# The zeroing of layer 1's expert slots, spread over more of the kernel

## The chip, the cores and the metric

One core of a Trainium2 chip runs the whole program: TensorE (PE; its weight loads are shown apart as PEld), VectorE (DVE), ScalarE (ACT), GpSimd (POOL), SyncE (SP), and 16 DMA engines that all of them feed. The metric is the time of one execution in device microseconds, here the median of several. An engine carries out its own instructions in order and waits by semaphore for what another one makes. A DMA is issued by SP, ACT or POOL and runs beside; whoever needs its data waits for its landing.

## The reference, cut to what matters

Two layers over `x` of 4 batches of 1024 tokens with 256 features, all in float32. Each layer norms its input, computes a sequence part `s` and a routed mixture of experts `g`, and adds `s * silu(g)`:

```python
xn = _layernorm(x)
s = _L0_attn_ref(xn, ...)             # a minimal GRU, a scan along the sequence
g = _silu(_L0_ffn_ref(xn, ...))       # 16 experts, hidden 128, 4 per token
x = x + s * g
xn = _layernorm(x)
s = _L1_attn_ref(xn, ...)             # attention over cos(theta) * cos(xn)
g = _silu(_L1_ffn_ref(xn, ...))       # 16 experts, hidden 64, 4 per token, plus a shared expert
x = x + s * g
```

The router takes, for each token, the two best of four groups of experts and then the four best experts in these; their scores, divided by their sum, weigh the four results.

## The kernel before

**Slots.** The tokens of an expert are brought together in DRAM. A group of tokens has an array `rows_in` with one row for each slot; an expert's tokens take whole tiles of 128 slots, so the number of slots is fixed and some stay empty. POOL scatters each token's row into its four slots with indirect DMAs (`scattered`, L577: 128 rows in one DMA). The expert loop then loads four tiles at a time (a quad), multiplies, and puts the results back. Layer 0 has two such groups of tokens (`HALVES`, 64 and 96 tiles), layer 1 has two as well (`GROUPS`, batches 0 and 1, then 2 and 3; 80 tiles each). The code numbers them 0, 1 and `G1` = 2, 3.

**Zeros.** Slots that no token takes must hold harmless rows, so each `rows_in` is filled before anything is scattered into it. `cleared(g, part, parts)` (L833) writes one part of a group's array from a tile of zeros, as one DMA on SP. Layer 0's two arrays are written whole, at the start. For layer 1 a row has 261 numbers (256 features, the marks of the token's four slots, and a result row; for an empty slot the last is a huge number), and an array is 10.7 MB; it is written in ten parts of 1044 KB each. `clears(10)` (L1325) yields the twenty parts one by one.

**Order of the work.** The order in which instructions stand on each engine is written by a planner in the code. A main loop (`run`, L887) advances a planning clock by a fixed amount for each of its steps (`PAIR` 0.81 for layer 0's experts, `ATTEND` 1.4, `SHARE` 2.6, `ROUTED` 0.64), and a few products of side work add their length to it (`spent`). After each step it lets side tasks go on (`Beside.advance`, L873), each of which is due again after the pause that it yields, times its pace. The clock decides the order only; nothing waits for it on the chip. The stages, with the planning clock worked out from these constants:

| stage | steps | planning clock |
|---|---|---|
| layer 0's routing, scatters, GRU | | 0 to 56.1 |
| layer 0's experts (`experts0`), 80 pairs of tiles | 333 x 0.81, and 24.3 of `spent` | 56.1 to 350.1 |
| attention and shared expert of batch 0 | 34 x 1.4 and 18 x 2.6, and 13.9 of `spent` | 350.1 to 458.4 |
| the same of batch 1 | the same, 10.3 of `spent` | 458.4 to 563.1 |
| the same of batch 2 | the same, no `spent` | 563.1 to 657.5 |
| layer 1's experts (`routed1`), 80 pairs | 0.64 a step | from 657.5 |
| shared expert and attention of batch 3 | | the end |

Beside layer 0's experts and the first three batches of attention run these tasks: `clearing` (the zeros: a part every `CLEAR` = 18.0, from 56.9 to 399.9), `combined` (it gathers layer 0's results with POOL, four indirect DMAs for 128 tokens, weighs them, L725 and L790 to L792, and writes layer 1's input), `routing` (layer 1's routing of the four batches, then `places1` of both groups, then `dispatch1(0)`, then `dispatch1(1)`), `weighing` and `preparing`.

**The scatters of layer 1.** `dispatch1(h)` first waits, in the planning clock, until all zeros have been issued (`while not clearing.done`). It then puts on POOL, for each of four pieces, a load of 512 tokens (`t_half`, L951), two small copies, and 16 scatters (L582), 20.3 planning units a piece. The last batch's routing is done at 502.3, so group `G1` is dispatched from 502.3 to 564.5 and the other group from 564.5 on. When the first is dispatched, `loads1` (L1370) puts the first three loads of layer 1's experts on SP (`xs<-rows_in`, L621), still at 564.5; these must wait until the group's scatters have landed. `weights1` (L960) follows each dispatch with 12 DVE instructions of 0.42 us for that group. Each scatter waits on the chip for every zero that was written to its own array.

**Layer 1's experts.** Each quad ends in a tile `o` of which there are three (`OB` = 3, shared by rotation). DVE writes the first half of it (L685), ACT the second (L679), and POOL stores its four tiles with four indirect DMAs (`results<-o,dest`, L1205). These stores stand behind all scatters in POOL's order. The fourth quad's first half can be written only when the first quad's stores have landed.

Of the kernel before, what the change touches and what calls it, by code (L numbers as in the profile page):

```python
# [52 lines left out]
PIECE = 1.0  # L53
# [3 lines left out]
CLEAR = 18.0  # L57
# [6 lines left out]
def two_layer_kernel(  # L64
# [33 lines left out]
    def block(dram, b, q):  # L98


        if len(dram.shape) == 4:
            return dram[b, q].rearrange("p (c d) -> p c d", c=NS)
        return dram[b].rearrange("(c p) d -> p c d", p=P)[:, q * NS : (q + 1) * NS, :]
# [383 lines left out]
    G1 = len(GROUPS)  # L487
# [89 lines left out]
    def scattered(views, tokens, row, c0):  # L577

        indirect(len(views))
        for i, view in enumerate(views):  # L580
            s, k = divmod(i, TOPK)
            nc.gpsimd.indirect_dma_start(  # L582
                out=view,
                out_offset=bass.IndirectOffsetOnAxis(ap=row[:, c0 + s, k : k + 1], axis=0),
                in_=tokens[:, s, :],
                in_offset=None,
            )
# [245 lines left out]
    def cleared(g, part, parts):  # L833


        n = NSLOT[g] // parts
        a = rows_in[g].rearrange("(p m) d -> p m d", p=P)[:, part * n : (part + 1) * n]
        source = zeros_of[g // G1].rearrange("p z d -> p (z d)")

        rows = a.rearrange("p (m z) d -> p m (z d)", z=zeros_of[g // G1].shape[1])  # L840
        nc.sync.dma_start(out=rows, in_=source.unsqueeze(1).to_broadcast(rows.shape))
# [92 lines left out]
        placed1.append((yield from places(em1[:, tiles_of(h), :], G1 + h, WE1, "tp")))  # L934

    def dispatch1(h):
        while not clearing.done:
            yield PIECE
        row, top, _ = placed1[h]
        pieces = [(b, q) for b in GROUPS[h] for q in range(NQ)]  # L940
        n = NS * TOPK
        views = dram_disjoint_views(rows_in[G1 + h], len(pieces) * n)

        tokens = {}
        for i in range(-AHEAD, len(pieces)):
            if i + AHEAD < len(pieces):
                j = i + AHEAD
                tokens[j] = t = xpool.tile([P, NS, D + INFO], F32, tag="x", name="t_half", bufs=XB)
                ts = slice(j * NS, (j + 1) * NS)
                b, q = pieces[j]  # L950
                nc.gpsimd.dma_start(out=t[:, :, 0:D], in_=block(normed, b, q))  # L951
                nc.gpsimd.tensor_copy(t[:, :, D : D + TOPK], top[:, ts, 0:TOPK])
                nc.gpsimd.tensor_copy(t[:, :, D + TOPK], result0[:, ts])
            if i >= 0:
                scattered(views[i * n : (i + 1) * n], tokens.pop(i), row, i * NS)
                while clock[0] < pool_free[0] - n * INDIRECT:
                    yield PIECE
        dispatched.add(h)
# [327 lines left out]
    stored, routed_done = set(), set()  # L1286
# [25 lines left out]
    def combine0(g):  # L1312
        while g not in stored:
            yield PIECE
        yield from gated0(g, *routed[g][0:2])
# [6 lines left out]
            yield from route1(b, tag)  # L1322
            routed_done.add(b)

    def clears(parts):  # L1325
        for g in (G1, G1 + 1):
            for i in range(parts):
                cleared(g, i, parts)
                yield CLEAR

    def then(*steps):
        for g in steps:
            yield from g

    def until(ready, *beside):

        while not ready():
# [3 lines left out]
                    other.advance(clock[0])  # L1341

    ready, turned, placed1, weights, dispatched, stored1 = {}, {}, [], [], set(), {}
    clearing = Beside(clears(10))
    combined = Beside(then(gru(xnTs[3], 3, ("side", "side"), True), *(combine0(g) for g in range(len(HALVES)))))
    routing = Beside(
        then(
            *(step for h, bs in enumerate(GROUPS) for step in (routes1(bs, "side"), places1(h))),
            *(dispatch1(h) for h in range(len(GROUPS))),
        )  # L1350
    )
# [106 lines left out]
```

## Time and profile before

| what | value |
|---|---|
| median of 3 runs | 1134.29 us (1133.79 to 1134.44) |
| the profiled execution's own time | 1132.03 us |
| its span | 1130.3 us |
| granted TensorE clock, mean | 0.957 |
| PE busy | 1029.2 us, 91% of the span |
| DVE, ACT, POOL busy | 652.7, 463.9, 564.4 us |
| zeros of layer 1 | 20 DMAs of 1044 KB, 14.5 us to landing (median) |
| gathers of layer 0's results | 128 DMAs, 6.1 us to landing (median) |
| scatters of layer 1 | 128 DMAs, 2.6 us to landing (median) |
| stores of layer 1's results | 160 DMAs, 3.3 us to landing (median) |

The profiled execution is 2.3 us below the median of the runs. A line of the timeline reads: start, length, engine, line of the kernel, operation, written tile <- read tiles, how many, and in brackets how long the engine had been idle and what ended that. `SPq` and `ACTq` are DMA issues; their length is that of the issue, not of the transfer. A line of waits reads: who waited at which line for whom: us in total, how often, the longest. Rows of the windows give the busy time (and count) of PE, PEld, DVE, ACT and POOL in a stretch, then the granted clock, the busy share of the 16 DMA engines and the GB/s moved. In the profile layer 0's experts run from about 145 to 451 us, attention and the shared expert of batches 0 to 2 from 451 to 790 us, layer 1's experts from 790 to about 1030 us.

### The profile page before, as it was taken

What the parts mean: (1) busy time and instruction counts of PE and PEld (TensorE: products, weight loads), DVE (VectorE), ACT (ScalarE), POOL (GpSimd) and SP (SyncE); (2) the same over time, 40 slices, a digit from 0 to 9 for tenths busy, and PEclk for the clock granted to TensorE, in tenths of its full rate; (3) what the DMA queues carried; (4) which work ended last, traced back from release to release, by engine and by line L of the source; (5) the groups of instructions that cost most, each with busy time, mean ns of one, the idle gap of its engine ahead of it and who ended that gap; (6) DMA issues with size and microseconds to landing.
All of it is one profiled execution on the core that took longest, in us unless ns stands there. A gap on an engine that the chain in (4) does not pass through costs nothing.

```text
span 1130.3 us, 16158 instructions
## 1 busy us (share of the span) xinstructions
PE 1029.2 (91%) x4928; PEld 765.9 (68%) x4928; DVE 652.7 (58%) x1967; ACT 463.9 (41%) x1028; POOL 564.4 (50%) x589
## 2 busy tenths in 40 slices
PE   5678699999899799979589999999999999999997
PEld 4245368888778688666357765776777777776675
DVE  4866963333688733067977884023733337776666
ACT  3345454444355444331223621221655555553132
POOL 1277377741770000377334677777756666776000
PEclk9868899999999899998699999999999999999999
DMA  8997569999999487997236553654555569994871
GB/s 338 401 410 265 172 191 324 308 310 250 313 346 263 136 215 189 342 246 196 84 119 217 181 175 130 215 196 158 179 170 186 190 215 351 359 332 145 274 242 38
DMA packets 118995, 264.82 MB, mean 234 GB/s; under 512 B 14208, under 2 KB 71680, under 8 KB 117632
## 3 DMA queue, kind: packets, MB, share of 16 engines
q1 hardware_dynamic: 78256, 138.79, 39.3%
q0 software_dynamic: 27264, 75.86, 19.9%
q10 hardware_dynamic: 13392, 49.14, 12.8%
q8 instruction: 43, 0.70, 0.3%
q14 instruction: 40, 0.33, 0.1%
HBM read 119.34 MB, written 144.39 MB: 233 GB/s over the span
## 4 chain that ended last, share of the span: by engine, by line
PE 64%; DVE 21%; DMA 7%; issue 3%; ACT 2%; POOL 2%; DVEq 0%; ACTq 0%; POOLq 0%
PE gu L642 14%; PE acc L667 10%; PE acc L1091 7%; PE tp L630 5%; PE gu L1138 4%; PE acc L1154 4%; PE mm L1138 4%; PE mm L1059 4%; DMA r<-rows_out,row 3%; PE tp L659 3%; PE acc L296 2%; DVE x_half L1243 2%; DMA rows_out<-o 2%; PE mm L514 1%; DVE stats L199 1%
## 5 line engine op out<-in xcount | busy, mean ns | idle before, releaser
L725 POOL DMA_INDIRECT r<-rows_out,row x128 | 130.6, 1021 | 237.5 <-issue 156.5
L642 PE MATMUL gu<-w_sb,xT 128*128 x1280 | 238.0, 329 | 1.5 <-ACT xT L634 0.9
L642 PEld LDWEIGHTS gu<-w_sb,xT 128*128 128x128 f32 x1280 | 193.9, 192 | 15.9 <-issue 2.2
L1205 POOL DMA_INDIRECT results<-o,dest x160 | 159.7, 998 | 76.9 <-issue 29.4
L582 POOL DMA_INDIRECT rows_in<-x_half,row x128 | 134.2, 1048 | 102.7 <-issue 52.4
L667 PE MATMUL acc<-w_sb,hT 128*128 (+1 forms) x640 | 180.1, 397 | 4.0 <-ACT hT L661 4.0
L469 DVE SCALAR_TENSOR_TENSOR h<-sg,gu 128x256 f32<-128x256 f32 (+1 forms) x160 | 56.0, 351 | 161.4 <-ACT sg L468 161.2
L582 POOL DMA_INDIRECT rows_in<-t_half,row x128 | 126.0, 985 | 40.6 <-issue 38.3
L667 PEld LDWEIGHTS acc<-w_sb,hT 128*128 128x128 f32 (+1 forms) x640 | 107.3, 189 | 31.9 <-issue 15.8
L1091 PE MATMUL acc<-val,es 128*128 128x256 f32 x512 | 127.9, 392 | 0.8 <-ACT es L1071 0.8
L634 ACT COPY xT<-tp 128x512 f32<-128x512 f32 x160 | 93.7, 586 | 73.8 <-PE tp L630 71.3
L1091 PEld LDWEIGHTS acc<-val,es 128*128 128x128 f32 x512 | 97.5, 198 | 24.3 <-issue 10.3
L630 PE MATMUL tp<-ident,xs 128*128 128x128 f32 x640 | 101.0, 281 | 0.0
L468 ACT ACTIVATE sg<-gu 128x256 f32<-128x256 f32 (+1 forms) x160 | 53.0, 331 | 113.7 <-PE gu L642 108.6
L630 PEld LDWEIGHTS tp<-ident,xs 128*128 128x128 f32 x640 | 74.4, 142 | 32.5 <-issue 18.1
L685 DVE COPY o<-acc 128x512 f32<-128x512 f32 x80 | 55.0, 688 | 61.4 <-PE acc L667 60.2
L659 PE MATMUL tp<-ident,h 128*128 128x128 f32 (+1 forms) x320 | 62.1, 276 | 10.1 <-DVE h L653 7.8
L1059 PE MATMUL mm<-projT 128*128 128x512 f32 (+3 forms) x192 | 70.0, 487 | 0.0
L661 ACT COPY hT<-tp 128x256 f32<-128x256 f32 (+1 forms) x160 | 58.5, 366 | 25.6 <-PE tp L659 23.8
L1138 PE MATMUL gu<-xnT,w_sb 128*128 128x512 f32 x128 | 61.7, 603 | 5.2 <-ACT val L1013 3.7
L1138 PE MATMUL mm<-xnT,w_sb 128*128 128x512 f32 x128 | 61.8, 608 | 0.3 <-DVE act L469 0.3
L1154 PE MATMUL acc<-w_sb,act 128*128 128x256 f32 x256 | 60.0, 380 | 1.2 <-DVE act L1148 1.2
(225 smaller groups left out, 1449.3 us busy)
## 6 DMA issues: line engine op xcount, KB each, us to landing
rows_in<-zeros SPq DMA_DIRECT2D x20, 1044.0 KB, 14.5
xs<-rows_in SPq DMA_DIRECT2D x40, 512.0 KB, 6.0
rows_out<-o ACTq DMA_DIRECT2D x40, 512.0 KB, 7.4
xs<-rows_in ACTq DMA_DIRECT2D x37, 522.0 KB, 4.0
r<-results SPq DMA_DIRECT2D x32, 512.0 KB, 5.3
rows_in<-zeros SPq DMA_DIRECT2D x1, 12288.0 KB
rows_in<-zeros SPq DMA_DIRECT2D x1, 8192.0 KB
w_sb<-in_w_dram SPq DMA_DIRECT2D x4, 1536.0 KB, 16.8
```

Source lines behind the costliest of these rows:

```text
L582: nc.gpsimd.indirect_dma_start(out=view, out_offset=bass.IndirectOffsetOnAxis(ap=row[:, c0 + s, k : k + 1], axis=0), in_=tokens[:, s, :], ...
L630: nc.tensor.transpose(tp[:, at : at + P], xs[:, j % per * 2 + i, kc * P : (kc + 1) * P], ident)
L634: nc.scalar.copy(xT.rearrange("p i k t -> p (i k t)"), tp)
L642: nc.tensor.matmul(ps[:, i * 2 * hid : (i + 1) * 2 * hid], lhsT=xT[:, i, kc, :], rhs=w_sb[:, bass.ds(off + kc * 2 * hid, 2 * hid)], start= ...
L659: nc.tensor.transpose(tp[0:hid, i * P : (i + 1) * P], h[:, i, :], ident)
L667: nc.tensor.matmul(ps[:, i * D : (i + 1) * D], lhsT=hT[0:hid, i * P : (i + 1) * P], rhs=w_sb[0:hid, bass.ds(expert(2 * j + i) + 4 * hid, D ...
L725: nc.gpsimd.indirect_dma_start(out=r[:, k, :], out_offset=None, in_=rows_out[g], in_offset=bass.IndirectOffsetOnAxis(ap=row[:, c, k : k + ...
L1059: nc.tensor.matmul(ps[:, at:TB], lhsT=projT[kc][:, t * P : (t + 1) * P], rhs=projT[kc][:, q * TB + at : (q + 1) * TB], start=(kc == 0), st ...
L1091: nc.tensor.matmul(av[s // 2][:, (s % 2) * D : (s % 2 + 1) * D], lhsT=es[:, s * P : (s + 1) * P], rhs=val[t // NS][:, t % NS, :], start=(t ...
L1138: nc.tensor.matmul(ps, lhsT=w[:, kc, j * P : (j + 1) * P], rhs=xr[:, kc, :], start=(kc == 0), stop=(kc == KC - 1),)
L1154: nc.tensor.matmul(ys[s // 2][:, (s % 2) * D : (s % 2 + 1) * D], lhsT=h[:, s * P : (s + 1) * P], rhs=ds1_sb[:, j, :], start=(j == 0 and s ...
L1205: nc.gpsimd.indirect_dma_start(out=views[g - G1][QUAD * q + i], out_offset=bass.IndirectOffsetOnAxis(ap=dest[:, i : i + 1], axis=0), in_=o ...
```

## The change

`clears` is now a task of one group. Group `G1`'s ten parts are spread at 36 planning units each; the second group's ten parts begin when layer 0's experts have been planned to their end (`1 in stored`) and the first group is through, and follow at 18 each. `dispatch1(h)` waits for the zeros of its own group (`clear_groups`) where it waited for both. The same twenty DMAs are issued, on the same queue, with the same contents.

```diff
     def dispatch1(h):
-        while not clearing.done:
+        while G1 + h not in clear_groups:
             yield PIECE
...
-    def clears(parts):
-        for g in (G1, G1 + 1):
-            for i in range(parts):
-                cleared(g, i, parts)
-                yield CLEAR
+    def clears(g, parts):
+        while g > G1 and 1 not in stored:
+            yield PIECE
+        for i in range(parts):
+            cleared(g, i, parts)
+            yield CLEAR if g > G1 else 2 * CLEAR
+        clear_groups.add(g)
...
-    clearing = Beside(clears(10))
+    clear_groups = set()
+    clearing = Beside(then(*(clears(g, 10) for g in (G1, G1 + 1))))
```

## The prediction, written before the result was known

> **What bounds the kernel now.** I read the page's slices of the span first, for where PE is not full and whether the DMA engines are full at the same time.
>
> ```profile
> PE   5678699999899799979589999999999999999997
> DMA  8997569999999487997236553654555569994871
> ```
>
> Each slice is 28.3 us. PE sets the time wherever it shows 9. In layer 0's experts (slices 5 to 15) the DMA engines are as full as PE and PE dips at slices 10 and 13; it dips again at 17, 19 and 20, where attention begins. The windows give these stretches exact edges.
>
> ```profile
> 282.00:311.00 29.00, 24.57 (x127) 20.83 (x125) 17.83 (x38) 11.39 (x27) 21.39 (x22) 0.94 1.01 308
> 370.00:396.00 26.00, 20.94 (x98) 17.53 (x97) 19.33 (x69) 11.53 (x21) 0.00 (x0) 0.87 0.54 149
> 480.00:516.00 36.00, 29.32 (x141) 24.16 (x139) 21.02 (x60) 10.04 (x30) 26.54 (x27) 0.88 0.96 254
> 535.00:571.00 36.00, 20.14 (x47) 11.47 (x45) 32.81 (x121) 10.83 (x16) 10.98 (x10) 0.76 0.24 70
> 720.00:790.00 70.00, 70.00 (x262) 47.17 (x261) 18.80 (x36) 14.98 (x40) 51.95 (x58) 1.00 0.57 200
> ```
>
> PE is idle 4.4, 5.1, 6.7 and 15.9 us in the first four rows. In the fourth DVE is full (32.8 of 36) and the DMA engines are not (0.24), so no transfer matters there. In the last PE has no gap. Next I read who waits for a transfer; first DVE's waits of 255 to 345, then those of 440 to 520.
>
> ```profile
> DVE y L792 <- DMA r<-rows_out,row: 4.1, 5, 2.3
> ```
>
> ```profile
> DVE y L792 <- DMA r<-rows_out,row: 6.8, 7, 2.8
> ```
>
> DVE waits for gathers of layer 0's results; with two short lists (0.8 at L790 there, 1.8 from 345 to 400) it is 13.5 us in all. This is what fewer zeros could shorten. Last come the queues that the change touches: SP's timeline, POOL's, and DVE's.
>
> ```profile
> 280.72 0.59 SPq L841 DMA_DIRECT2D rows_in<-zeros  x1
> ...
> 457.66 13.01 SPq L841 DMA_DIRECT2D rows_in<-zeros  x1
> ...
> 477.90 0.59 SPq L841 DMA_DIRECT2D rows_in<-zeros  x1
> ...
> 509.40 0.63 SPq L841 DMA_DIRECT2D rows_in<-zeros  x1
> ...
> 656.57 0.32 SPq L1040 DMA_DIRECT2D attended<-sv  x1
> 719.23 1.34 SPq L621 DMA_DIRECT2D xs<-rows_in  x3
> 740.87 14.30 SPq L1040 DMA_DIRECT2D attended<-sv  x2
> ```
>
> ```profile
> 716.04 0.96 POOL L582 DMA_INDIRECT rows_in<-t_half,row  x1 [0.31 <-issue]
> ...
> 722.54 1.03 POOL L582 DMA_INDIRECT rows_in<-t_half,row  x1 [2.36 <-issue]
> ...
> 804.13 0.96 POOL L582 DMA_INDIRECT rows_in<-t_half,row  x1 [0.30 <-issue]
> 805.40 0.96 POOL L1205 DMA_INDIRECT results<-o,dest  x1 [0.30 <-DVE projT L181]
> ```
>
> ```profile
> 818.07 0.69 DVE L685 COPY o<-acc 128x512 f32<-128x512 f32 x1 [1.27 <-PE acc L667]
> ...
> 831.91 0.69 DVE L685 COPY o<-acc 128x512 f32<-128x512 f32 x1 [9.55 <-PE acc L667]
> ```
>
> SP issues nothing from 657 to 719: the three tile loads of layer 1's experts wait there for the first group's last scatter (716.04). POOL is without a gap from 633 to 820: first group's scatters, the second's (722.5 to 805.1), then result stores. DVE's copy at 818.07 is the first half of the fourth quad; it needs the first quad's `o` back.
>
> **The change part by part.** The sum is made against the profiled execution, 1132.03 us, 2.3 below the median; I add the difference to the median, 1134.29.
>
> *Where the zeros come to stand.* By the planning clock the first group's ten parts start at 56.9 and follow at 36: nine stand within layer 0's experts (to 350), the tenth at 382, and the group is through at 423. They take every second place of before: 280.72 stays, 261.60 and 306.17 go; 477.90 stays, 457.66 and 509.40 go. The second group starts at 423 (just before layer 1's norm of batch 2 is stored, about 571 us) and follows at 18, with a few tenths of rounding each: part 8 at 550, part 9 at 568.7, part 10 at 586.9, through at 605. The first three tile loads are written to SP at 564.5. So two zeros come to stand behind them on SP, and the second group's scatters wait for both.
>
> *Removed from layer 0's experts and from the start of attention.* By 516 us, ten of twenty zeros are gone: 10.7 MB, at the 308 GB/s of the first window 35 us of the DMA engines. What it is worth is bounded by DVE's 13.5 us of waiting for gathers, and from below by nothing: a wait may be the gather's own latency. Of the 4.9 us before 345, nearly all falls at 294 to 301, in the wake of the zero of 280.72, which stays; of the 1.8 after 345, the zero of 343.50 goes. I take 2.0 for the two. Of the 6.8 after 440, one of the two zeros that stand there (457.66 and 477.90) goes, and SP's 13 us block at 457.66 may pass to the load behind it: half, 3.0. Sum: -5.0 us, range 0 to -13.5. The zero of 509.40 is worth nothing: DVE waits for no gather after 520.
>
> At this place a page speaks against any gain. The Trainium skill, "DMA: Bandwidth & Descriptors", section "Queues, rings and completion order", says that each DMA engine serves the queues that have work in turn, a packet at a time. By that a gather on POOL's queue would lose only a few packets to a zero on SP's, the first term would be near 0 and the sum +11.5. The chain of waits has gathers of 9.86 us (issued at 280.96) and 11.73 us (475.51) against a median of 6.1, so here more is lost, and I keep the row.
>
> *First group's own wait.* `dispatch1(0)` waits for half of the zeros now. Before, all had been issued at 509.4, and POOL's first load for it (623.51) waited 14.2 us for a DVE reader and 4.7 for a store of `normed`. Not binding: 0.
>
> *Second group's first eight zeros, beside attention.* Ten SP issues of 0.45 us move past SP's stores of `x1`, `normed` and `attended` and the reload of `xnT` (611.96). Same queue, so those land later by up to one zero, 1.07 MB or about 3.5 us. The `normed` store that POOL waits for was issued at 623.52, over 10 us after the nearest zero; `xnT` is first read at 624.61, 12.6 us after its issue. PE has no transfer on its path from 571 to 790. Cost 0; 2 us if the reload's cover is too short. Zeros 5 to 8 go out between 652 and 658, while POOL scatters; POOL's pace in the full stretch from 200 to 240 (31 in 40.2 us, 1.30 each) against 1.27 here says under 1 us.
>
> *The new wait.* Queued behind it: SP issues the three loads at 719.23, the two zeros at 720.6 and 721.0. The loads land after 8.4 us, at 728.5, sharing the engines with POOL's three loads of `normed`. The zeros follow on the same queue: 2.1 MB at 342 GB/s (the highest of the full windows, 311 to 340) is 6.2 us, so not before 734.8; with the shortest landing of that tensor, 2.4 us, 737.2. From above: the median landing of a zero, 14.5 us, on top of 728.5, 743. I take 738, near the lower end, because nothing else large moves then (DMA 0.57 in 720 to 790). The first scatter of the group moves from 722.5 to 738: 15.5 us (12.3 to 20.5). POOL's loads of `normed` stand before the waiting scatter and do not move; behind it stand 64 scatters and all 160 result stores, and all of them move by 15.5. The by-page price: "DMA: Bandwidth & Descriptors", section "Measured", gives 6.15 us for 1 MB, so two zeros end at about 741 and the sum would be about 3 us more.
>
> *Who waits for POOL.* The first quad's four stores go out from 805.40 at 1.27 each, the last at 809.2, and land 3.3 us later, 812.5. The fourth quad's copy at 818.07 has 5.6 us of margin. 15.5 - 5.6 = 9.9 us by which DVE stops, then ACT, then PE: DVE is in order, and the projections that PE's next products need (L998 at 818.95) stand behind the copy. Range 6.7 to 14.9. It is not made good: from here PE makes a quad in 5.7 us (the spacing of POOL's groups of four stores after 832) and POOL stores one in 5.07 (four times 1.27), so POOL catches up and PE, full to 1030, ends later by the stop. The second group's tile loads come only about 17 quads after 793.5, at 890, and its scatters now end at 821: 70 us of margin.
>
> *The clock after the stop.* After the gap of 4.25 us at 302.5 the next round of PE (302.54 to 307.41) took 4.87 us against 3.25 usual: +1.6. I take 1.6 here too, range 0 to 2.5. *Weights.* 12 DVE instructions of 0.42 us, 5.0 in all, move with the dispatch from batch 2's shared expert to the first quads, where DVE is busy 19.3 of 25 us (797 to 822). They lie inside the 9.9 us for which DVE would wait anyway: 0; without that wait up to 5.
>
> Sum: -5.0 + 9.9 + 1.6 = +6.5 us: 1138.5 for a profiled execution, 1140.8 for the median; I say 1140.5.
>
> **The rivals.**
>
> 1. *The stalls on gathers go whole* (faster). Place: 282 to 516 us. For it: the DMA engines show 0.95 to 1.05 there. All 13.5 us are won, and part of the granted clock of 0.94, 0.87 and 0.88, which costs 1.7, 3.4 and 4.3 us in the windows shown, say half, 4.7: -18.2 + 11.5 = -6.7, 1127.6. It decides from a gain of 11.5 us on. Against it: every second zero stays, among them those of 280.72 and 477.90.
> 2. *No new wait.* If SP took the last two zeros ahead of the tile loads, they would land before 716 and only the gain stays: 1129.3. Against it: the planning clock, 564.5 against 568.7 and 586.9, though the first margin is 4 units.
> 3. *A longer wait.* If the two zeros take the longest landing seen for one, 31.2 us from 720.6, the scatters start at 751.8, POOL is 29.3 us late and PE stops for 23.7: +20.3, 1154.6. For it: that landing occurred, with full DMA engines; against it, they are not full here.
> 4. *Gain and loss cancel.* The low end of the stop (6.7 + 1.6) and a gain of 8: 1134.6.
>
> **How the numbers follow.** About 0.2% (2.3 us) is what a measurement of this kernel can tell from no change. My forecast 0.60, with 1136.6 to 1147 as its own range (gain 8 to 2, stop 8.7 to 13); rival 1 0.10, rival 2 0.05, rival 3 0.10, rival 4 0.15. Faster 0.15, same 0.15, slower 0.70. A range from 1130 to 1150 leaves out most of rivals 1 to 3, about 0.2.
>
> **What the next profile would show.** SP: three tile loads, then two zeros at once, near 720. POOL: a gap of some 15 us between the two groups' scatters, ended by the landing of a zero; result stores from about 820. DVE: a copy at L685 that waits about 10 us for `results<-o,dest`, and PE idle as long near 820 to 830. DVE's waits for `r<-rows_out` under 13.5 us. The start of layer 1's experts a few us before 790. I am wrong if SP issues all zeros before its long wait, if the copy finds its `o` free, or if layer 0's experts end over 10 us sooner.

## The result, and the profile after

The changed kernel takes 1144.24 us (median of 4 runs, 1142.62 to 1144.91) where the kernel before takes 1134.37 beside it (1133.79 to 1135.99): a ratio of 1.0081, 95% interval 1.0058 to 1.0104. It is slower by 9.9 us; 1140.5 was predicted, with 1130 to 1150 as the range. The profiled execution took 1144.02 us (span 1142.3, granted clock 0.951), 12.0 us more than the one of before, which lies 2.3 us below its own median. The slices of the span (28.6 us each):

```profile
PE   5678699999899899987698999999699999999997
DMA  8997549988995484963477994864455668994782
```

Counted from 0, PE's dips at slices 13, 17 and 19 are a little smaller than before and the one at 10 is as it was; those at 18 and 21 are new, and so is the one at 28, in layer 1's experts. The windows, with the edges used before and two more (600 to 640, 790 to 835), have PE, PEld, DVE, ACT and POOL busy, then the granted clock, the DMA share and GB/s:

```profile
282.00:311.00 29.00, 26.30 (x143) 22.14 (x142) 22.44 (x59) 12.95 (x30) 20.64 (x22) 1.00 1.05 341
480.00:516.00 36.00, 31.95 (x139) 24.04 (x138) 24.11 (x79) 9.63 (x27) 28.08 (x27) 0.91 0.68 202
600.00:640.00 40.00, 35.02 (x148) 26.39 (x146) 33.43 (x114) 15.62 (x38) 13.16 (x18) 0.91 0.81 232
790.00:835.00 45.00, 32.42 (x177) 25.43 (x176) 24.73 (x73) 20.29 (x39) 34.60 (x35) 0.81 0.52 170
```

The last two of them in the kernel before:

```profile
600.00:640.00 40.00, 39.61 (x186) 30.51 (x185) 32.62 (x119) 16.89 (x40) 17.60 (x22) 0.96 0.61 209
790.00:835.00 45.00, 41.28 (x252) 32.51 (x252) 25.81 (x78) 26.89 (x53) 29.24 (x30) 1.00 0.52 172
```

So PE gains in the first two stretches and loses 4.6 us in the third and 8.9 us in the fourth, there with a lower clock besides. How far the same instruction of the changed kernel is from its place of before, along the run, gives the ledger:

| place in the kernel before | shift, us | in this stretch |
|---|---|---|
| x1's first store, 310.2 | -4.9 | -4.9 |
| end of layer 0's experts (load of shared weights on SP, 453.76) | -5.6 | -0.7 |
| x1's fifth store, 556.5 | -11.1 | -5.5 |
| x1's seventh store, 611.5 | -10.0 | +1.1 |
| x1's eighth store, 636.2 | -4.7 | +5.3 |
| last store of batch 2's shared expert, 792.6 | -4.3 | +0.4 |
| first half of the fourth quad, 818.07 | +8.6 | +12.9 |
| first half of the fifth, 831.91 | +10.5 | +1.9 |
| end of the span | +12.0 | +1.5 |

The waits behind three of these rows, of the kernel after: DVE's list from 255 to 345 and from 440 to 520 us, DVE's timeline near 604, PE's near 615.

```profile
DVE y L792 <- DMA r<-rows_out,row: 1.6, 4, 0.5
```

```profile
DVE y L792 <- DMA r<-rows_out,row: 2.0, 1, 2.0
```

```profile
604.67 0.35 DVE L790 TENSOR_SCALAR y<-r,wk 128x256 f32<-128x256 f32 x1 [3.19 <-DMA normed<-y]
```

```profile
615.32 0.69 PE L235 MATMUL tp<-ident,y 128*128 128x128 f32 x2 [4.59 <-ACT y L226]
```

The waits for gathers have gone from 13.5 to 4.2 us (with 0.3 at L790 in either list, and none from 345 to 400). But at 604 DVE now waits to overwrite `y`, because the store of `normed` that reads it has not landed; then ACT and PE wait. Near 720 the queues look as predicted. SP, POOL and DVE after:

```profile
589.95 0.45 SPq L841 DMA_DIRECT2D rows_in<-zeros  x1
590.49 2.04 SPq L916 DMA_DIRECT2D normed<-y  x1
...
715.53 1.28 SPq L621 DMA_DIRECT2D xs<-rows_in  x3
716.86 6.19 SPq L841 DMA_DIRECT2D rows_in<-zeros  x2
```

```profile
738.12 1.04 POOL L582 DMA_INDIRECT rows_in<-t_half,row  x1 [20.88 <-DMA rows_in<-zeros]
...
820.33 0.96 POOL L1205 DMA_INDIRECT results<-o,dest  x1 [0.30 <-issue]
```

```profile
826.64 0.69 DVE L685 COPY o<-acc 128x512 f32<-128x512 f32 x1 [9.82 <-DMA results<-o,dest]
```

Three tile loads, two zeros behind them, POOL's scatter that waits for a zero's landing, result stores 14.9 us late, and the copy that waits for `o`: the chain of the forecast, in its order.

### The profile page after: what moved, and what is told of

It is laid out like the page before. It is cut to its first block, busy times and chain, and to the rows that moved or that the text cites. A ratio compares the mean times of both kernels' runs of the same rounds, so it can differ in the third digit from the quotient of the medians.

```text
span 1142.3 us, 16159 instructions
## 1 busy us (share of the span) xinstructions
PE 1034.2 (91%) x4928; PEld 768.8 (67%) x4928; DVE 652.0 (57%) x1967; ACT 463.6 (41%) x1028; POOL 564.4 (49%) x589
## 4 chain that ended last, share of the span: by engine, by line
PE 55%; DVE 18%; POOL 10%; DMA 8%; issue 6%; ACT 2%; SPq 0%; DVEq 0%; ACTq 0%; POOLq 0%
PE gu L642 14%; PE acc L667 11%; POOL rows_in L582 9%; PE tp L630 6%; PE acc L1091 4%; PE tp L659 3%; PE mm L1059 2%; DMA rows_in<-t_half,row 2%; PE gu L1138 2%; PE acc L1154 2%; PE acc L296 2%; DMA rows_in<-zeros 2%; DMA r<-rows_out,row 2%; PE mm L514 1%; DVE stats L199 1%
## 5 line engine op out<-in xcount | busy, mean ns | idle before, releaser
L582 POOL DMA_INDIRECT rows_in<-x_half,row x128 | 133.6, 1044 | 103.9 <-issue 55.2
L659 PEld LDWEIGHTS tp<-ident,h 128*128 128x128 f32 (+1 forms) x320 | 37.7, 128 | 36.6 <-issue 20.4
```

What stands on the lines that cost most here:

```text
L582: nc.gpsimd.indirect_dma_start(out=view, out_offset=bass.IndirectOffsetOnAxis(ap=row[:, c0 + s, k : k + 1], axis=0), in_=tokens[:, s, :], ...
L659: nc.tensor.transpose(tp[0:hid, i * P : (i + 1) * P], h[:, i, :], ident)
```

## The experiments

Two theories stood at the start. The queue theory: two zeros behind the tile loads make POOL late, and that costs the time. The rival: zeros beside attention and the first group's scatters cost it, wherever the last two stand. Two questions came up on the way: why 11 us were won where 5 were forecast, and what was lost at 604.

### No zero behind the tile loads

The second group's parts follow at 0.72 of the pause, so that all ten stand ahead of the loads:

```diff
-            yield CLEAR if g > G1 else 2 * CLEAR
+            yield 0.72 * CLEAR if g > G1 else 2 * CLEAR
```

> The second group's zeros follow at 13 planning units in place of 18, so all ten stand on SP ahead of the three tile loads; nothing else is changed against the changed kernel (1144.2). Theory Q (the two zeros that stood behind the tile loads made POOL late): POOL's gap between the two groups' scatters goes back to some 6 us, DVE's copy at the fourth quad does not wait for its tile, and the time is that of before less the 4.3 us by which layer 1's experts began earlier: 1129 to 1132. Rival C (the zeros beside attention slow other transfers, and the late scatters are only one sign of it): they are as many and closer together here, so 1142 to 1147.

1125.65 us (1122.55 to 1126.96) against 1134.49, ratio 0.9921 (0.9896 to 0.9946): faster than both kernels. SP and POOL of this run:

```profile
657.07 11.65 SPq L841 DMA_DIRECT2D rows_in<-zeros  x2
711.86 1.35 SPq L621 DMA_DIRECT2D xs<-rows_in  x3
```

```profile
715.06 1.04 POOL L582 DMA_INDIRECT rows_in<-t_half,row  x1 [2.27 <-issue]
```

POOL has no gap between the groups, and DVE waits 0.9 us in all for `o` (13.7 in the changed kernel). The loss at 604 is absent too: x1's eighth store is 9.6 us ahead of before. That is how it can be better than expected. Not all of it lasts: batch 2's last shared store is 7.6 us ahead and the end of the span 5.1; what takes the rest is not shown.

### The wait alone

The kernel before, with the last two zeros of the second group held until the tile loads stand on SP; the other eighteen keep their places. Each dispatch waits for its own group.

```diff
     def dispatch1(h):
-        while not clearing.done:
+        while G1 + h not in clear_groups:
             yield PIECE
...
     def clears(parts):
         for g in (G1, G1 + 1):
             for i in range(parts):
+                while g > G1 and i >= parts - 2 and 0 not in dispatched:
+                    yield PIECE
+                if g > G1 and i == parts - 2:
+                    yield 2 * PIECE
                 cleared(g, i, parts)
                 yield CLEAR
+            clear_groups.add(g)
...
+    clear_groups = set()
     clearing = Beside(clears(10))
```

> The kernel before, with only its last two zeros held back until the tile loads stand on SP, and each group's scatters waiting for its own zeros. Eighteen zeros stay where they were. Theory Q: SP gets free at 719 as before, the zeros land near 740, POOL and the fourth quad stop for 12 to 15 us, nothing is won: 1146 to 1150. Rival C: two zeros fewer beside layer 0's experts and none beside attention, so no slower than before: 1132 to 1135.

1142.49 us (1142.05 to 1143.25) against 1134.49, ratio 1.0082 (1.0056 to 1.0109). POOL:

```profile
743.55 1.19 POOL L582 DMA_INDIRECT rows_in<-t_half,row  x1 [21.10 <-DMA rows_in<-zeros]
```

DVE waits 14.5 us for `o`, and the clock of 790 to 835 is 0.86. So the wait by itself costs 8 us, without any change to the other zeros; the queue theory is right as to the cause and 3.5 us too high, at its lower end, as to its size.

### The last zeros on another queue

The second group's zeros are issued by ACT, so that nothing stands behind the tile loads on SP.

```diff
-        nc.sync.dma_start(out=rows, in_=source.unsqueeze(1).to_broadcast(rows.shape))
+        (nc.scalar if g > G1 else nc.sync).dma_start(out=rows, in_=source.unsqueeze(1).to_broadcast(rows.shape))
```

> The changed kernel with layer 1's second group's zeros issued by ACT in place of SP, at the same places of the plan. Theory Q: ACT is not held up by the tile loads, so the last two zeros land before 712 us and POOL's gap goes: 1129 to 1133. If it is the place in the plan (after the dispatch of the first group), and not SP's order, that makes them late: 1142 to 1146. Rival C: the same transfers at nearly the same times, so 1142 to 1146.

1143.22 us (1140.81 to 1143.48), ratio 1.0079 (1.0051 to 1.0108): no better than the changed kernel. ACT carries out its own work in order and comes to the last two zeros at 705.85 and 728.39; the first scatter starts at 736.75 after a wait of 16.88 (the profile puts the end of this wait down to DVE, which had long been done, not to a zero). So it is not SP's blocked queue alone that matters but the place in the order: what is planned behind the loads comes late on ACT as well, which is in step with attention.

### One zero behind, and three

The pause is 0.9 of the changed kernel's, then 1.24.

```diff
-            yield CLEAR if g > G1 else 2 * CLEAR
+            yield 0.9 * CLEAR if g > G1 else 2 * CLEAR
```

> The second group's zeros follow at 16.2 units: one stands behind the tile loads where there were two. Theory Q: POOL's gap of 20.9 us shortens by one zero's transfer, 3 to 6 us, and the time by as much: 1138 to 1141. Rival C: 1143 to 1145.

1140.55 us (1138.05 to 1143.49), ratio 1.0064 (1.0037 to 1.0091), as expected. The first scatter starts at 735.22, 2.9 us sooner than with two, after a wait of 15.67 us (20.88 with two), so most of the wait comes with the first zero behind the loads.

```diff
-            yield CLEAR if g > G1 else 2 * CLEAR
+            yield 1.24 * CLEAR if g > G1 else 2 * CLEAR
```

> The second group's pause is 1.24 times the changed kernel's, so three zeros stand behind the tile loads on SP, the second and third of them also behind one and two stores of batch 2's attention, which SP can issue at about 740 and 755 us only. Theory: the second group's scatters, the result stores behind them and the copy at the fourth quad move with the landing of the last zero. That is then near 760 where it was 738; the stop grows by 22 us less what little slack is left: the time is 1160 to 1168 us. Rival: the loss at the fourth quad does not follow the last zero's landing but comes from the amount moved beside attention: with one zero fewer ahead of the loads, 1140 to 1145 us.

1157.48 us (1150.68 to 1160.93), ratio 1.0193 (1.0133 to 1.0253): 2.5 us below the range, and by another road. The last zero went out at 753.54 and POOL's scatter waited 44.00 us, to 765.51. But the planner now put the first result stores between the scatters (16 stores after the group's first 32 scatters, 48 more after the next 16), so the fourth quad's copy stood at 818.5, where it was before the change. The cost came later, in PE's timeline:

```profile
936.05 1.09 PE L630 MATMUL tp<-ident,xs 128*128 128x128 f32 x4 [15.70 <-DMA xs<-rows_in]
```

There PE waits for the second group's first tile; the group's last 16 scatters go out from 910 to 929.

### The first dispatch waits for all zeros again

```diff
     def dispatch1(h):
-        while G1 + h not in clear_groups:
+        while not clearing.done:
```

> The changed kernel with one part undone: both dispatches wait in the planning clock for all twenty zeros, as before the change; the zeros keep their new places in the planning clock. On SP all ten of the second group's zeros then stand ahead of the three tile loads, and the tile loads stand behind the two stores of batch 2's attention (740 and 755 us). Theory: the harm at the fourth quad comes from the two zeros behind the tile loads alone. Then POOL has no gap between the two groups' scatters, the tile loads land near 765, 25 us before layer 1's experts need them, the loss at 600 to 640 stays, and the time is 1128 to 1131 us. Rival: the spread itself, with zeros beside attention and the scatters, makes the scatters late whatever the wait: then the time stays within 1138 to 1146. If the tile loads come too late, layer 1's experts start after 790 and the time is above 1134.

1187.54 us (1184.44 to 1189.95), ratio 1.0485 (1.0432 to 1.0539). Both theories missed. The gap of 15 us was gone, and the fourth quad's copy came 1.7 us ahead of before. But the planner reaches the second dispatch so late that only 16 of its 64 scatters stand ahead of the result stores. The other 48 stand behind 64 of the first group's 80 stores and run from 899 to 960; POOL is idle for 56.94 us before its first result store at 797.50. PE pays:

```profile
965.46 1.09 PE L630 MATMUL tp<-ident,xs 128*128 128x128 f32 x4 [55.08 <-DMA xs<-rows_in]
```

With the zeros spread this far, the wait for one's own group is what keeps the second group's scatters ahead of the stores.

### No zero beside the last gathers

The second group's zeros start when both groups' slots are placed, and follow at 5 units.

```diff
-        while g > G1 and 1 not in stored:
+        while g > G1 and len(placed1) < len(GROUPS):
             yield PIECE
...
-            yield CLEAR if g > G1 else 2 * CLEAR
+            yield 5.0 if g > G1 else 2 * CLEAR
```

> The first group's zeros are spread as in the changed kernel; the second group's ten are held until both groups' slots have been placed (planning clock 502) and then follow at 5 units, so none is issued beside the gathers and stores of 560 to 615 us, and all ten stand ahead of the tile loads on SP. Theory: the changed kernel lost 6.6 us at 600 to 640 because a zero issued at 589.95 held up gathers of layer 0's last results. Then here the 11 us won up to 601 are kept, DVE has no wait for a gather and PE no stall near 615, POOL has no gap before the second group's scatters, the fourth quad's copy comes near 808 and the time is 1122 to 1125 us. Rival: ten zeros cost wherever they stand beside POOL's transfers; here they stand beside the first group's scatters (628 to 715), which then end later than 720, or the zeros land later than 722, and the time is 1127 to 1133 us. If the loss at 600 to 640 comes from something else than the zeros, PE's stall near 615 stays and the time is that of the kernel with the second group's pause cut to 0.72, 1125 to 1127 us.

1138.67 us (1136.52 to 1140.54) against 1133.50, ratio 1.0054 (1.0030 to 1.0078). The first half of the theory held: x1's eighth store follows the seventh by 24.6 us, as before the change. But the burst cost more than the rival allowed. SP and POOL:

```profile
652.86 61.29 SPq L841 DMA_DIRECT2D rows_in<-zeros  x7
721.67 3.12 SPq L621 DMA_DIRECT2D xs<-rows_in  x3
```

```profile
733.10 1.04 POOL L582 DMA_INDIRECT rows_in<-t_half,row  x1 [16.85 <-DMA rows_in<-zeros]
```

SP needs 61 us to get seven zeros out (DMA share 1.07 from 680 to 720), and they land after 722 although they stand ahead of the loads. Batch 2's attention waits as well: ACT stands for 9.18 us up to 708.87 and PE for 5.83 up to 709.61. That makes the time here, not POOL's gap: batch 2's last shared store comes 3.5 us later than before the change, and DVE waits only 0.6 us in all for `o`.

### What the zero at 589.95 costs

The changed kernel, with the second group's second part held back by up to 4 units, so that it stands behind the store of `normed`:

```diff
         for i in range(parts):
+            late = 4 if g > G1 and i == 1 else 0
+            if late:
+                yield late
             cleared(g, i, parts)
-            yield CLEAR if g > G1 else 2 * CLEAR
+            yield CLEAR - late if g > G1 else 2 * CLEAR
```

> The changed kernel with the second part of the second group's zeros, and the parts behind it, held back by up to 4 planning units: on SP the zero that the chip issued at 589.95 now stands behind the stores of normed (590.5) and of its turned copy (592.6), not ahead of them; two zeros still stand behind the tile loads. Theory: the 5.3 us lost between 602 and 636 come from that store landing late behind a zero on the same queue (DVE's wait of 3.19 for normed, PE's of 4.59). Then DVE has no wait for normed at 604, PE no stall of over 2 us near 615, xnT is issued near 604 and batch 2's attention begins 10 us earlier than before the change, where it was 4.7. Rival: the loss is contention of zeros with the gathers: then a stall of 3 us or more stays. As to the end: if the whole chain moves with it, 1137 to 1141 us; if the last two zeros still land at 738, because the zeros of 640 to 700 now stand closer together, the end stays at 1142 to 1145 us.

This run, the even spacing and the half period came to a chip on which the kernel before takes 1474.36 us (clock 0.85; 1134 on the others). In the profiles taken there engines stood for tens of us, PE up to 40.3, without anything in the profile that released them. 1458.16 us, ratio 0.9877 (0.9813 to 0.9942), says nothing of the 1134 us kernel's end, and that part stays open. The local question it does answer: no wait of DVE for `normed`, and x1's eighth store 24.7 us after the seventh. The line of `normed`'s store in the DMA view (size, us from issue to landing), before and in the changed kernel:

```profile
normed<-y SPq DMA_DIRECT2D x1, 512.0 KB, 7.2
```

```profile
normed<-y SPq DMA_DIRECT2D x1, 512.0 KB, 14.0
```

Over the profiles:

| kernel | last zero ahead of `normed`'s store | store lands after | x1's seventh to eighth store |
|---|---|---|---|
| before | none near | 7.2 us | 24.7 us |
| pause 0.72 | 12 us ahead | 9.1 | 24.6 |
| late burst | none near | 6.9 | 24.6 |
| this one | moved behind it | not read | 24.7 |
| changed | 0.5 us ahead, SP | 14.0 | 30.0 |
| on ACT | 2.1 us ahead, ACT's queue | 14.2 | 28.3 |

The kernels with 0.9, 1.24 and the first dispatch's old wait have a zero 0.5 us ahead as well: 29.8, 30.6 and 30.5 us (the store lands after 14.6 and 15.0 in the first two). So with a zero just ahead of it, on the same queue or on another, the store takes twice as long to land, and DVE's rewriting of `y` pays for it.

### Why 11 us were won: density or place

Twenty zeros evenly, and the first group's half a period later with the second group's pause at 0.6:

```diff
-        while g > G1 and 1 not in stored:
-            yield PIECE
         for i in range(parts):
             cleared(g, i, parts)
-            yield CLEAR if g > G1 else 2 * CLEAR
+            yield 1.35 * CLEAR
```

> All twenty zeros evenly, one in 24.3 planning units, with no condition on layer 0's experts; the last stands ahead of the tile loads; per-group wait as in the changed kernel. If the time lost on gathers of layer 0's results depends on how dense the zeros are, the density between that of before (18) and that of the changed kernel (36, from 423 on 18) gives between half and all of the 11 us won by 545 us: x1's fifth store 6 to 11 us earlier than before the change. No zero stands right ahead of a store of normed between 575 and 625, and three stand between 630 and 715 where the kernel with the pause of 0.72 has five: no loss of over 2 us to 790, no gap on POOL. Time 1122 to 1128 us. Rival: only half the density in layer 0's experts avoids their stalls: under 4 us are won, 1128 to 1132 us.

```diff
+        if g == G1:
+            yield CLEAR
         for i in range(parts):
             cleared(g, i, parts)
-            yield CLEAR if g > G1 else 2 * CLEAR
+            yield 0.6 * CLEAR if g > G1 else 2 * CLEAR
```

> The changed kernel with the first group's zeros half a period later (the first at 74.9 planning units, then each 36), so that of the zeros of before 261.60 and 306.17 stay and 280.72 goes, the other half of what the change kept; the second group's pause is 0.6 times, so that all of them stand ahead of the tile loads. It asks why DVE's waits of 294 to 301 and PE's stall at 302 went although the zero of 280.72 stayed. If the density did it (two zeros 19 us apart), the stall is gone here too, DVE's waits for gathers of 255 to 345 stay under 2.5 us and x1's second store (337.1 before the change) comes 4 to 6 us earlier. If the one neighbour that the change took away did it (261.60, just ahead of the gathers), the stall is back: waits of 3 us or more and 0 to 3 us won there. Time 1123 to 1129 us, with no gap on POOL, if nothing new stands ahead of a store that somebody waits for.

On the chip of 1474 us: 1466.54 (ratio 0.9934, 0.9889 to 0.9978) and 1467.08 (0.9929, 0.9879 to 0.9979), which tells nothing of the question. Both were run once more on another chip.

> The kernel with the first group's zeros half a period later and the second group's pause of 0.6 once more, on a chip where the kernel before takes its usual 1134 us. If the density of the zeros made the stall at 294 to 302 (two of them 19 us apart), the stall is gone here too: DVE's waits for gathers of 255 to 345 under 2.5 us, x1's second store (337.1 before the change) 4 to 6 us earlier. If the one neighbour that the change took away did it (261.60, just ahead of the gathers), waits of 3 us or more are back and x1's second store is 0 to 3 us earlier. Between batch 2's third and fourth x1 stores 24 to 25 us, as no zero stands right ahead of normed's store there (30 us in the changed kernel). No gap on POOL at 715. Time 1123 to 1129 us.

> The kernel with twenty zeros evenly at 24.3 units once more, on a chip where the kernel before takes its usual 1134 us. By the density: half to all of the 11 us are won by 545 us (x1's fifth store 6 to 11 us earlier), no loss of over 2 us to 790, no gap on POOL, 1122 to 1128 us. Rival: only half the density in layer 0's experts avoids their stalls: under 4 us are won, 1128 to 1132 us.

The half period: 1131.09 us (1126.95 to 1135.19) against 1134.23, ratio 0.9965 (0.9940 to 0.9990), 2 us above its range; the second of its two readings held, with waits of 4.0 us and x1's second store 1.7 us ahead. Batch 2's third and fourth x1 stores (the seventh and eighth in all) were 25.5 us apart, where 24 to 25 was expected. Even spacing: 1135.05 (1129.13 to 1140.81), ratio 1.0008 (0.9978 to 1.0039). The rival's small gain came (x1's fifth store 2.8 us ahead), and at the end not even that was left. The first gather of layer 0's results, in the changed kernel, then with the half period, then with even spacing:

```profile
273.68 0.99 POOL L725 DMA_INDIRECT r<-rows_out,row  x1 [31.88 <-PE tp L630]
```

```profile
279.06 0.99 POOL L725 DMA_INDIRECT r<-rows_out,row  x1 [40.26 <-DMA xs<-rows_in]
```

```profile
277.85 0.99 POOL L725 DMA_INDIRECT r<-rows_out,row  x1 [37.60 <-DMA xs<-rows_in]
```

The gathers need the first group's results; the last of its sixteen stores is issued by ACT at 267.5 before and within 1.2 us of that in the others. A zero goes out some 6 us ahead of it, at 261.60 before, 260.61 with the wait alone, 261.05 and 260.43 in these two, and is still under way (14.5 us to landing, median); the changed kernel has none there. The line of that last store in the DMA view, before and in the changed kernel:

```profile
rows_out<-o ACTq DMA_DIRECT2D x1, 512.0 KB, 9.9
```

```profile
rows_out<-o ACTq DMA_DIRECT2D x1, 512.0 KB, 5.5
```

It lands 10.7 us after its issue with the half period and 10.0 with the wait alone; the view has no landing for the even spacing. In these four kernels the first gather starts 0.9 to 1.0 us after this landing. (The profile puts the gather's wait down to a tile load or to PE; that the store ends it follows from the code and from these times.) Before (278.39), in the kernel with the wait alone (277.6) and in these two the first gather starts at 277.6 to 279.1; in the six runs on these chips that keep the changed kernel's first group, and in the changed kernel, at 272.9 to 273.9. The end of layer 0's experts goes with it: the half period has as few zeros as the changed kernel and yet loads the shared weights at 453.62, as before the change (453.76); the six runs load them at 448.5 to 451.1. So this part of the gain, 5.6 us in the changed kernel and 2.7 to 5.3 in the six, does not come from the density. That it is the place of this one zero is what all these profiles agree with; no run moved that zero alone. The zero near 280 costs something too: from the first gather to x1's first store it is 31.9 us before, 31.6 in the changed kernel and 28.4 with the half period, which has no zero there. By its third store of x1 the half period has lost this again (0.1 us ahead); where is open.

DVE's waits of 255 to 345 agree (4.9 us before, 4.0 with the half period, 5.4 even, 1.9 after). The waits of 440 to 520 follow what stands there: 6.8 us with the zeros of 457.66 and 477.90, 3.6 with one of 457.51, 4.7 with one of 459.91 (the wait alone), 7.1 with those of 454.93 and 482.70, 2.3 with one of 469.07. From the load of the shared weights to x1's fifth store it is 102.7 us before, 100.6 with the wait alone, 100.1 with the even spacing, 96.9 with the half period, and 96.9 to 98.4 in the changed kernel and the six runs.

## Why the prediction was right, and where it was wrong

*Removed from layer 0's experts and from the start of attention*: -5.0 forecast, -11.1 measured by x1's fifth store, inside the range to -13.5. What failed is the sentence that nearly all of the first wait falls in the wake of the zero of 280.72, which stays, and so the 2.0 for layer 0's experts: 5.6 measured. The runs point to the zero of 261.60, under way with the last store of results that the gathers wait for, and that one goes. The 3.0 for the start of attention measured 5.5. The page held against the gain there (the Trainium skill, "DMA: Bandwidth & Descriptors", section "Queues, rings and completion order") was laid to the wrong transfer. By the same rule, as an estimate, a store of 512 KB beside a zero of 1044 KB on another queue would get about half of the turns. A landing of 14.2 us where it was 7.2 fits that; the same queue gave 14.0, and no run shows the shares.

*Second group's first eight zeros, beside attention*: 0 forecast, 2 if the reload's cover is too short; 5.3 measured between x1's seventh and eighth store. This step looked for who reads what the late stores write (POOL, and the reload of `xnT`) and had no row for who overwrites their source: DVE's next `y`. The two misses nearly cancel, by luck: batch 2 ends 4.3 us early, where 5.0 was forecast.

*The new wait*: right in mechanism and place. Landing at 738 was forecast and 738.12 is the start of the scatter; that it is so close is luck, by two sizes that were off against each other. The loads were issued 3.7 us sooner than the 719.23 that I held fixed, and the scatter started 21.3 us after the first zero's issue, not 17.4. Their rate was mis-sized; the DMA view of the kernel after, first 716 to 727, then 727 to 735, where the zeros are alone:

```profile
DMA packets 1426, 3.97 MB, mean 361 GB/s; under 512 B 112, under 2 KB 587, under 8 KB 1425
```

```profile
DMA packets 1498, 1.54 MB, mean 193 GB/s; under 512 B 22, under 2 KB 1498, under 8 KB 1498
```

At 193 GB/s two zeros take 11.1 us, not the 6.2 that 342 GB/s gave. The same page's section "Measured" states 6.15 us for 1 MB, there for a load from HBM issued by GpSimd. Twice that, 12.3 us as an estimate, comes nearer to the 11.1.

*Who waits for POOL*: 9.9 us forecast, 12.9 measured at the fourth quad's copy. The margin of 5.6 holds; the lateness was taken against the places of before. A landing at 738 meets a stage that has moved 4.3 us forward, and the stores' 14.9 us late are 19.2 for it: 19.2 - 5.6 = 13.6. The gain ahead of a wait that does not move with it is lost in the wait, and the sum counted it in full. Without the -5.0 the forecast's own terms give +11.5 for the profiled execution, where 12.0 was measured: this is the step that failed. PE's share looks different from the forecast: it stands 3.06 and 5.79 us, not some 10 in one piece, and runs at half clock between and after. *Weights*: 0 held. Most of their instructions ran from 808.7 to 814.4, with DVE full and PE standing for the 3.06 us, but the stores held the copy until 826.64 in any case.

*The clock after the stop*: 1.6 forecast, 1.9 measured between the fourth and the fifth quad's copies (clock 0.52 from 815 to 822, 0.53 from 825 to 836). That stretch also holds a wait of PE of 1.92 us for ACT, and part of the slow clock lies ahead of it, so the clock's own share is not separated. *First group's own wait*: 0 held. A further 1.5 us to the end, with four shorter waits for `o` (13.7 us in all, 9.8 of them the first), was not forecast. In sum, by the ledger: -4.3 + 12.9 + 1.9 + 1.5 = +12.0 for the profiled execution against +6.5.

Of the rivals, the second (no new wait) is the kernel with the pause of 0.72, with 1125.65 where 1129.3 was worked out. The first had most of its gain (11.1 us by x1's fifth store, with 9.3 of the 13.5 us of waiting gone), and the wait outweighed it. A landing as late as the third one's 31.2 us did not occur.

## What to carry to other kernels

A filler transfer was priced here by its neighbours more than by its share of the traffic: look at which transfers are under way with it, ask who reads that transfer and also who overwrites its source, and move the filler there first. Where a transfer is moved across the point at which a later stage's loads are written, everything that waits for it is late with those loads, on SP's queue and on ACT's; here that alone cost 8 us, and 5 planning units less between two zeros turned a loss of 9.9 us into a gain of 8.8. When gains come ahead of such a wait, subtract them from its margin before they are summed.

## What the runs showed of the hardware

- Zeros in rows of 1044 bytes moved, from 727 to 735 in the changed kernel, at 193 GB/s with the DMA engines full (share 1.07 of 16 engines on SP's queue), mixed loads just before at 361: a full DMA share does not tell the rate.
- A store of 512 KB landed 14.0 us after its issue with a zero 0.5 us ahead on the same queue, 14.2 with one 2.1 us ahead on another, and 7.2 without.
- SP's issue itself stood for 61.29 us over seven zeros of 1044 KB, and 6.19 over two behind three loads; everything behind on the queue waits with it.
- Around stalls of PE of 3.06 us (to 816.53) and 5.79 us (to 828.29) the granted clock was 0.52 from 815 to 822 and 0.53 from 825 to 836, with 1.00 between them.
- One of the chips ran the unchanged kernel in 1474 us, 30% slower; in the profiles of three other kernels taken there PE stood up to 40.3 us without a releaser, at a clock of 0.85 to 0.86. Why is open.
